# Constant rows copied by the engines that fill the first attention operands, and another order at the end of a four-stage transformer kernel

## The chip, the cores and the metric

The kernel runs on one core of a Trainium2 chip, as one program. A core has five engines that run their own instruction streams and wait for each other by semaphores: TensorE (PE, matrix products into PSUM, with its weight loads shown as PEld), VectorE (DVE), ScalarE (ACT), GpSimd (POOL) and SyncE (SP). SP, ACT and POOL also issue DMAs, and a DMA that waits for something holds up what its engine issues behind it. Sixteen transfer engines move the data of all queues. The metric is the time of one execution in microseconds (us), less is better.

## The reference

The input x holds 8 sequences of 512 tokens with 128 features, in fp32. Four stages follow each other, each with a sum of its input and its output and a layer norm behind it:

```
x = layernorm(x + attn0(x))   # 16 heads of 8; softmax(q k / sqrt(8) - slope_h |i - j|) v
x = layernorm(x + ffn0(x))    # silu(gate) * up, all operands quantised to FP4 in blocks of 16
x = layernorm(x + attn1(x))   # 16 heads of 8, without the distance term
x = layernorm(x + ffn1(x))
```

ffn1 is itself two layers. Each takes h, which is x with the second half of the features moved on by one token; makes q, k, v for 8 heads of 64; scales q and k to unit length, turns them with rotary tables; attends within a window of 64 tokens back; adds the projection to x; shifts again, normalises, and adds `(a * gelu(g)) @ w2 + b2` with `a, g` from one product of inner size 341 each.

## The kernel before, in words

**Stages and names.** x stays on the chip as xn and xs, 128 tokens a tile, four tiles (NT) a sequence, B = 8 sequences. Matrix products and transpositions of the attention are recorded by the helpers mm (L262) and tr (L263); the calls of the other engines show as L48 in the first stages and as L655 in ffn1, where the helper `kept` holds each engine to the program's order. `held` (L79) and `held_a` (L80) issue DMAs on SP's and ACT's queues in program order.

**The first attention's operands.** For each sequence there are two tiles q and k of 128 x 8 x 512 in the matrix format fp32r: eight pairs of heads in the middle dimension, and 64 partitions for each head of a pair (j = 0, 1). Of the 64 partitions, 0 to 31 hold data: the high and the low part of q and k, in the combinations whose products give an almost exact score. Partitions 32 to 47 hold constants that make the distance term, `rowq` and `rowk`; partition 63 holds a constant -1 in k and, in q, the largest score of each row, which is put there later (mt, by POOL's queue). The rest is zero. There are two sets: q0, k0 for even sequences and q1, k1 for odd ones.

Before the first sequence, `begin_x` transposes x (xt_ps, xT), `begin_qk` projects it for q and for k (qk_ps, x), POOL splits x in two parts, and SP writes these to a buffer in DRAM called far, two DMAs for each of q and k. `load_qk` reads them back spread over the partitions: 24 DMAs for q on SP and 24 for k on ACT. `begin_v` makes the values (va). Then the scores s_ps start: VectorE takes their row maxima m (sixteen large reductions for a group), these go back as mt, and a second product t_ps (the transposed scores), the exponential e and the product av with the values follow. A planner (`later`) hands the other sequences' operand steps, the bias row `crow` and the later stages' weights to numbered steps of this loop.

**The constants before.** DVE sets q0 to zero and POOL k0, while ACT's queue loads `raw`, 17 rows of 2 x 512; DVE casts it into rowq and rowk; then `constant_rows(0, held)` issues six DMAs on SP: row 63 of k, rows 32 to 47 of q and of k, for j = 0 and 1, each with its source broadcast over the eight pairs (16 KB or 256 KB written). They stand on SP's queue ahead of the far DMAs. `first_late`, called once when the first operands have been begun, does the same for q1 and k1: a memset on DVE and one on POOL, the values' ones (`filled`), six more row DMAs, and then `load_late`, the loads of x for sequences 2 to 7.

**The end of the last stage.** ffn1 has K = 16 items (layer times sequence) of NT = 4 chunks of 128 tokens: LAST = 64 chunks. A loop handles chunk t's projections together with the later steps of chunks t-1 to t-5: `operands_T` and `operands` (kT, qT copies), `scores` (sp), `maxima` (m), `weights` (pw, eight exponentials with sums on ACT), `over_sums` (POOL's product of pw with the reciprocal den), `weights_T` and `weights_taken` (p_ps, pT), `values` and `values_taken` (o_ps, oT), and `sums` (the products y_ps and their addition to xs by DVE). When an item's four chunks are summed, `shifted` (L709) builds hn, the shifted copy, by a small memset and four DMAs on SP (112 rows, 15 rows, the row that passes from a tile to the next, and the unshifted half); `normed` takes its moments (bn and st on DVE, rstd and mr on POOL) and adds the bias and x to xs (two POOL additions); `scaled` normalises hn; `turned` transposes it (nT); `gated` makes gelu and product of one of three parts (gp, ap, u); `sums(LAST, ..)` multiplies u by w2.

The loop leaves the last steps to a tail that is written out by hand (L1087 to L1148). In it E = 14 and L = 15 are the last two items. `rest(t)` issues the remaining steps of four chunks at once in a fixed order; `measured` and `finished` are the final layer norm of a sequence whose layer 1 is complete, with its output DMA.

```
E, L = K - 2, K - 1
rest(LAST)
sums(LAST - 5, LAST - 11)
begin_hn(E)
rest(LAST + 1)
normed(E)
...
begin_hn(L)
finished(E - 1 - B)
```

Of the kernel before, what the change touches and what calls it, by code (L numbers as in the profile page):

```python
# [9 lines left out]
F32 = mybir.dt.float32  # L10
F32R = mybir.dt.float32r
# [7 lines left out]
P = 128  # L19
B, S, D = 8, 512, 128  # L20
NT = S // P
# [30 lines left out]
def body(ctx, tc, x, consts, rows, wa0, wa1, acols, bo, wf, wqkv, wo, w1, w2, cols, b2r, qs, ks, out):  # L52
    nc = tc.nc
# [8 lines left out]
    rowq = outer.tile([16, S], F32R, name="rowq")  # L62
    rowk = outer.tile([17, S], F32R, name="rowk")
    sel = outer.tile([P, 2 * P], BF16, name="sel")
# [24 lines left out]
    dve.memset(half, -0.5)  # L89
    dve.memset(q0.bitcast(F32), 0.0)  # L90
    pool_.memset(k0.bitcast(F32), 0.0)
    with tc.tile_pool(name="rw", bufs=1) as once:
        raw = once.tile([17, 2, S], F32, name="raw")
        held_a(out=raw, in_=rows)
        held_a(out=wa[0], in_=wa0)
        held_a(out=acol, in_=acols)
        dve.tensor_copy(rowq, raw[0:16, 0, :])
        dve.tensor_copy(rowk, raw[:, 1, :])
    dve.tensor_tensor(qb, acol[:, :, 0], acol[:, :, 1], ALU.mult)
    dve.tensor_copy(sel, cst[:, C_SEL : C_SEL + 2 * P])  # L100
    dve.tensor_copy(tri, cst[:, C_TRI : C_TRI + P])
# [154 lines left out]
    def attention(li, alibi, qs_, ks_, va, batch, late=None, spare=None, alone=0):  # L256
# [7 lines left out]
        with ExitStack() as st:  # L264
# [137 lines left out]
            def plan():  # L402
# [34 lines left out]
                if not begun:  # L437
                    begin_x(0, batch[0])
                    begin_qk(0, batch[0], 0, held)
                    begin_qk(0, batch[0], 1, held)  # L440
                    begin_v(0, batch[0])
                    for part in (slice(0, 2), slice(2, 4), 1):
                        load_qk(0, batch[0], 0, part, held)
                        load_qk(0, batch[0], 1, part, held_a)
# [9 lines left out]
                if late:  # L454
                    late()
                if spare:
# [194 lines left out]
    def ffn1():  # L651
# [20 lines left out]
        LAST = NT * K  # L672
# [36 lines left out]

        def shifted(src, h):  # L710

            p_set(h[0:1, 0, 64:128], 0.0)
            for at, n in ((0, 112), (112, 15)):
                nc.sync.dma_start(out=h[at + 1 : at + 1 + n, :, 64:128], in_=src[at : at + n, :, 64:128])
            nc.sync.dma_start(out=h[0:1, 1:NT, 64:128], in_=src[P - 1 : P, 0 : NT - 1, 64:128])
            nc.sync.dma_start(out=h[:, :, 0:64], in_=src[:, :, 0:64])
            return h

        def rows_of(k):
            return slice((k % B) * NT, (k % B + 1) * NT)  # L720
# [70 lines left out]
        def main():  # L791
            with ExitStack() as st:
# [136 lines left out]

                def values_taken(k, c, h):  # L930
                    h["oT"] = work.tile([P, 4, P], F32, tag="oT", name="oT")
                    copy(h["oT"], h.pop("o"))

# [40 lines left out]

                def normed(k):
                    l, x = k // B, xs[:, rows_of(k), :]
                    item[k]["shape"] = moments(item[k]["hn"], "h")
                    p_tt(x, x, b2[:, l, :].unsqueeze(1).broadcast_to([P, NT, D]), ALU.add)
                    if l:
                        p_tt(x, x, xn[:, rows_of(k), :], ALU.add)  # L980
# [24 lines left out]
                def finished(b):  # L1005
                    x = slice(b * NT, (b + 1) * NT)
                    normalized(xs[:, x, :], xn[:, x, :], item[B + b].pop("shape"))
                    nc.sync.dma_start(out=ov[:, b], in_=xn[:, x, :])
# [67 lines left out]

                def rest(t):
                    at_(t - 4, weights_T)
                    at_(t - 3, over_sums)
                    at_(t - 4, weights_taken)  # L1080
                    at_(t - 2, scores)
                    at_(t - 2, maxima)
                    at_(t - 2, v_of)
                    at_(t - 1, operands_T)
                    at_(t - 1, operands)
                    at_(t - 4, values)
                    at_(t - 2, weights)  # L1087
                    at_(t - 4, values_taken)

                def begin_hn(k):  # L1090
                    hn = work.tile([P, NT, D], F32, tag="hn", name="hn", bufs=1)
                    item[k]["hn"] = shifted(xs[:, rows_of(k), :], hn)
# [40 lines left out]
                scaled(L)  # L1133
                for z in range(4):
# [20 lines left out]
    with tc.tile_pool(name="ops", bufs=1) as ops:  # L1155
        qs_, ks_ = ([at, ops.tile([P, 8, S], F32R, name=f"{n}1")] for n, at in (("q", q0), ("k", k0)))
        def constant_rows(i, start):
            for j in range(2):
                for t, at, src in ((ks_[i], 63, rowk[16:17]), (qs_[i], 32, rowq), (ks_[i], 32, rowk[0:16])):
                    n = src.shape[0]  # L1160
                    start(
                        out=t[64 * j + at : 64 * j + at + n].bitcast(F32),
                        in_=src.bitcast(F32).unsqueeze(1).broadcast_to([n, 8, S]),
                    )

        va = [va0, ops.tile([P, NT, 16, 32], F32, name="va1")]
# [49 lines left out]
        second, gates = [], []  # L1216
        constant_rows(0, held)
        psum = ExitStack()
# [25 lines left out]
def _constants():  # L1244
# [25 lines left out]
    at, blk = np.arange(S) - S // 2, np.arange(S) // 64  # L1270
    rows = np.zeros((17, 2, S), np.float32)
# [4 lines left out]
    rows[16, 1] = -1.0  # L1276
    return c, rows
# [55 lines left out]
```

## Time and profile before

The time is 1720.63 us, the median of three runs (1718.25 to 1721.07).

| what | value |
|---|---|
| profiled execution | 1720.81 us |
| its span, first to last instruction | 1719.0 us |
| mean granted TensorE clock | 0.972 |
| TensorE busy | 1620.5 us, 94% |
| VectorE busy | 1373.8 us, 80% |
| ScalarE busy | 1242.5 us, 72% |
| GpSimd busy | 911.6 us, 53% |
| moved by DMA | 90.25 MB, mean 53 GB/s |

Lines of a profile are read so. A line of the timeline or of the chain of waits gives the start in us from the start of the span, the length in us, the engine or DMA queue (SPq is SyncE's), the line of the code, and output<-input by the program's names; x4 means four such in a row, and brackets give the idle time before and what ended it. The chain of waits follows the work that ended last back through what released it. In a table by stretches, each engine has its busy time and number of instructions; then come TensorE's granted clock (1.00 is full), the busy share of the transfer engines and GB/s.

### The profile page before, as it was taken

How to read it: one execution, taken by the hardware profiler on the slowest of the kernel's cores; microseconds unless marked ns; L12 is line 12 of the kernel's file. 1: busy time of each engine (PE TensorE's matmuls, PEld its weight loads, DVE VectorE, ACT ScalarE, POOL GpSimd, SP SyncE). 2: the span in 40 equal slices, each digit the busy share in tenths (PEclk: the TensorE clock that was granted, in tenths of full speed). 3: DMA queues.
4: the chain of work that ended last, by engine and by line, in shares of the span. 5: the costliest groups of instructions: out<-in, count | busy, mean ns of one | idle time of the engine just before them, and what ended most of it. 6: DMA issues, size and time to landing. Idle time of an engine off the chain costs nothing.

```text
span 1719.0 us, 41770 instructions
## 1 busy us (share of the span) xinstructions
PE 1620.5 (94%) x16177; PEld 936.5 (54%) x16177; DVE 1373.8 (80%) x2177; ACT 1242.5 (72%) x2980; POOL 911.6 (53%) x976
## 2 busy tenths in 40 slices
PE   4999999999988799999999989999999999999995
PEld 2454555545546544444444446666666666666664
DVE  4788877888749878988889848888888888888863
ACT  1577776777755558887778767787888878888883
POOL 3323332232236741332332258888888888888873
PEclk7899999999999979999999999999999999999998
DMA  6725232221110243332332101111111111111110
GB/s 126 165 61 150 61 63 52 64 53 25 15 14 1 74 79 73 71 68 62 75 66 36 45 7 41 34 36 35 36 40 37 38 38 36 44 42 41 35 35 26
DMA packets 80777, 90.25 MB, mean 53 GB/s; under 512 B 46098, under 2 KB 58386, under 8 KB 76611
## 3 DMA queue, kind: packets, MB, share of 16 engines
q1 hardware_dynamic: 75504, 85.52, 23.2%
q8 instruction: 129, 2.11, 0.5%
q10 hardware_dynamic: 978, 1.52, 0.4%
q0 software_dynamic: 4096, 0.54, 0.3%
q14 instruction: 70, 0.57, 0.1%
HBM read 41.85 MB, written 18.87 MB: 35 GB/s over the span
## 4 chain that ended last, share of the span: by engine, by line
PE 78%; DVE 7%; POOL 5%; ACT 5%; issue 2%; DMA 2%; SPq 0%; DVEq 0%; POOLq 0%; ACTq 0%
PE av L262 16%; PE s_ps L262 13%; PE t_ps L262 10%; PE y_ps L655 5%; PE sp L655 5%; PE o_ps L655 3%; PE t_ps L655 3%; PE v_ps L655 3%; PE p_ps L655 3%; PE q_ps L655 3%; PE k_ps L655 2%; PE gp L655 2%; PE ap L655 2%; PE qk_ps L262 2%; ACT e L48 2%
## 5 line engine op out<-in xcount | busy, mean ns | idle before, releaser
L48 DVE TENSOR_REDUCE m<-s_ps 128x2 f32<-128x1024 f32 x512 | 620.4, 1223 | 140.7 <-PE s_ps L262 138.1
L48 ACT ACTIVATE e<-t_ps 128x512 f32<-128x512 f32 x1024 | 555.9, 596 | 166.1 <-PE t_ps L262 156.3
L262 PE MATMUL av<-e,va 128*32 128x256 f32 x4096 | 328.9, 394 | 6.8 <-ACT avs L48 6.8
L262 PE MATMUL s_ps<-k,q 63*128 63x512 f32 x1024 | 264.4, 510 | 21.5 <-DMA q<-far 15.1
L48 POOL DMA_DIRECT2D q<-mt x128 | 68.9, 542 | 347.7 <-ACT mt L48 347.3
L262 PE MATMUL t_ps<-q,k 64*128 64x512 f32 x1024 | 248.9, 447 | 1.3 <-ACT e L48 1.3
L655 ACT ACTIVATE pw<-sp,m,was_v 128x128 f32<-128x128 f32 x512 | 227.4, 480 | 1.5 <-DVE m L655 0.9
L262 PEld LDWEIGHTS s_ps<-k,q 63*128 63x128 f32 x1024 | 99.3, 188 | 228.3 <-issue 157.4
L655 POOL TENSOR_TENSOR was_v<-was_v 128x16 f32<-128x16 f32 x64 | 187.6, 2931 | 5.3
L262 PEld LDWEIGHTS t_ps<-q,k 64*128 64x128 f32 x1024 | 122.9, 189 | 23.7 <-ACT e L48 10.9
L262 PEld LDWEIGHTS av<-e,va 128*32 128x32 f32 x4096 | 81.6, 108 | 96.3 <-issue 62.7
L655 POOL TENSOR_TENSOR pw<-pw,den 128x1024 f32<-128x1024 f32 x64 | 121.2, 1894 | 9.3 <-DVE den L655 9.3
L655 ACT ACTIVATION_READ_ACCUMULATOR pw<-sp,m,was_v 128x1 f32 x512 | 116.5, 228 | 0.0
L262 PEld LDWEIGHTS <-sel 64*128 64x128 bf16 x2048 | 66.8, 97 | 76.4 <-issue 54.4
L655 DVE TENSOR_REDUCE m<-sp 128x4 f32<-128x512 f32 x128 | 82.2, 683 | 22.0 <-PE sp L655 20.2
L48 POOL CAST parts<-x 128x512 fp32r<-128x512 f32 x32 | 19.4, 608 | 139.8 <-ACT x L48 139.8
L655 POOL TENSOR_TENSOR was_k<-was_k,was_q 128x512 f32<-128x512 f32 x64 | 88.0, 1375 | 5.3 <-DVE was_q L655 5.3
L655 ACT COPY v<-v_ps 128x512 f32<-128x512 f32 x64 | 37.6, 588 | 72.3 <-PE v_ps L655 72.3
L655 PEld LDWEIGHTS t_ps<-cst,was_k 128*128 128x128 f32 x512 | 59.7, 142 | 43.1 <-issue 22.5
L655 DVE COPY pT<-p_ps 128x512 f32<-128x512 f32 x128 | 79.9, 664 | 0.5 <-PE p_ps L655 0.5
L655 PEld LDWEIGHTS p_ps<-cst,pw 128*128 128x128 f32 x512 | 59.8, 141 | 33.1 <-issue 27.8
L655 DVE TENSOR_REDUCE was_v<-was_k 128x16 f32<-128x1024 f32 x64 | 77.0, 1204 | 0.0
(191 smaller groups left out, 3223.1 us busy)
## 6 DMA issues: line engine op xcount, KB each, us to landing
far<-parts SPq DMA_DIRECT2D x64, 256.0 KB
q<-far SPq DMA_DIRECT2D x248, 64.0 KB
k<-far SPq DMA_DIRECT2D x240, 64.0 KB
ve<-v SPq DMA_DIRECT2D x112, 128.0 KB
xn<-in_x SPq DMA_DIRECT2D x8, 256.0 KB
q<-mt POOLq DMA_DIRECT2D x128, 4.0 KB, 3.0
hn<-xs SPq DMA_DIRECT2D x16, 128.0 KB
hn<-xs SPq DMA_DIRECT2D x16, 112.0 KB
```

What stands on the lines that cost most here:

```text
L48: return lambda *a, **k: self.tc.keep_in_program_order(f(*a, **k))
L262: mm = lambda *a, **k: tc.keep_in_program_order(nc.tensor.matmul(*a, **k))
L655: kept = lambda f: lambda *a, **k: tc.keep_in_program_order(f(*a, **k))
```

## The change

**Constants at the start.** The host's rows become 32 x 2 x 512 (sixteen constants, fifteen zero rows, and the last, -1 for k). The first 1024 columns of wqkv_s, a tile for weights that are loaded much later, serve as a buffer `fixed` of 128 x 2 x 512. DVE sets it to zero; ACT's queue loads the weights wa0, acol, crow, and then the rows twice, into partitions 32 to 63 and 96 to 127 of `fixed`. DVE copies its q half into q0, broadcast over the eight pairs (4096 elements a partition); ACT copies the k half into k0, between `begin_qk` and `begin_v`; POOL copies both into q1 and k1 in `late(True)`. rowk, the casts, the four memsets of the tiles and the twelve row DMAs are gone.

**The end of ffn1.** The `rest` calls are written out and reordered. The sum of chunk LAST-5 and hn's DMAs for E come ahead of the transposed operands of LAST-1; the weights of LAST-2 come ahead of kT and qT on ACT; the moments of hn(E) come behind the weights of LAST-1; one copy of oT goes to DVE; POOL's two additions for E (`based`) go behind `begin_hn(L)`; the four DMAs of hn(L) are split, two on SP and two on ACT's queue; and `finished` of sequence 5 goes behind the gelus of E.

```diff
-    dve.memset(q0.bitcast(F32), 0.0)
-    pool_.memset(k0.bitcast(F32), 0.0)
-    with tc.tile_pool(name="rw", bufs=1) as once:
-        raw = once.tile([17, 2, S], F32, name="raw")
-        held_a(out=raw, in_=rows)
-        held_a(out=wa[0], in_=wa0)
-        held_a(out=acol, in_=acols)
-        dve.tensor_copy(rowq, raw[0:16, 0, :])
-        dve.tensor_copy(rowk, raw[:, 1, :])
+    fixed = wqkv_s.rearrange("p l f -> p (l f)")[:, 0 : 2 * S].rearrange("p (n t) -> p n t", n=2)
+    dve.memset(fixed, 0.0)
+    held_a(out=wa[0], in_=wa0)
+    held_a(out=acol, in_=acols)
+    for j in range(2):
+        held_a(out=fixed[64 * j + 32 : 64 * j + 64], in_=rows)
+    filled_with = lambda e, t, n: e.tensor_copy(t, fixed[:, n, :].unsqueeze(1).broadcast_to([P, 8, S]))
     dve.tensor_tensor(qb, acol[:, :, 0], acol[:, :, 1], ALU.mult)
+    filled_with(dve, q0, 0)
...
                     begin_qk(0, batch[0], 1, held)
+                    late(False)
                     begin_v(0, batch[0])
...
-                    late()
+                    late(True)
...
-        def shifted(src, h):
+        def shifted(src, h, start=nc.sync.dma_start, other=None):
+            other = other or start
             p_set(h[0:1, 0, 64:128], 0.0)
-            for at, n in ((0, 112), (112, 15)):
-                nc.sync.dma_start(out=h[at + 1 : at + 1 + n, :, 64:128], in_=src[at : at + n, :, 64:128])
-            nc.sync.dma_start(out=h[0:1, 1:NT, 64:128], in_=src[P - 1 : P, 0 : NT - 1, 64:128])
-            nc.sync.dma_start(out=h[:, :, 0:64], in_=src[:, :, 0:64])
+            for at, n, by in ((0, 112, start), (112, 15, other)):
+                by(out=h[at + 1 : at + 1 + n, :, 64:128], in_=src[at : at + n, :, 64:128])
+            other(out=h[0:1, 1:NT, 64:128], in_=src[P - 1 : P, 0 : NT - 1, 64:128])
+            start(out=h[:, :, 0:64], in_=src[:, :, 0:64])
...
                 def normed(k):
+                    item[k]["shape"] = moments(item[k]["hn"], "h")
+                    based(k)
+
+                def based(k):
                     l, x = k // B, xs[:, rows_of(k), :]
-                    item[k]["shape"] = moments(item[k]["hn"], "h")
                     p_tt(x, x, b2[:, l, :].unsqueeze(1).broadcast_to([P, NT, D]), ALU.add)
...
                 E, L = K - 2, K - 1
-                rest(LAST)
+                at_(LAST - 4, weights_T)
+                at_(LAST - 3, over_sums)
+                at_(LAST - 4, weights_taken)
+                at_(LAST - 2, scores)
+                at_(LAST - 2, maxima)
+                at_(LAST - 2, v_of)
                 sums(LAST - 5, LAST - 11)
-                begin_hn(E)
-                rest(LAST + 1)
-                normed(E)
+                begin_hn(E, held)
+                at_(LAST - 1, operands_T)
+                at_(LAST - 2, weights)
+                at_(LAST - 1, operands)
+                at_(LAST - 4, values)
+                at_(LAST - 4, values_taken)
+                at_(LAST - 3, weights_T)
+                at_(LAST - 2, over_sums)
+                at_(LAST - 3, weights_taken)
+                at_(LAST - 1, scores)
+                at_(LAST - 1, maxima)
+                at_(LAST - 1, v_of)
+                at_(LAST - 3, values)
+                at_(LAST - 1, weights)
+                item[E]["shape"] = moments(item[E]["hn"], "h")
+                at_(LAST - 3, values_taken, v_copy)
+                sums(LAST - 4, LAST - 10)
+                turned_over(LAST - 2)
+                at_(LAST - 2, values)
+                at_(LAST - 1, over_sums)
+                at_(LAST - 2, values_taken)
                 scaled(E)
-                sums(LAST - 4, LAST - 10)
-                rest(LAST + 2)
                 sums(LAST - 3, LAST - 9)
-                measured(E - 1)
+                turned_over(LAST - 1)
                 turned(E)
                 turned_taken(E)
-                rest(LAST + 3)
+                at_(LAST - 1, values)
+                at_(LAST - 1, values_taken)
                 sums(LAST - 2, LAST)
                 sums(LAST - 1, LAST)
-                begin_hn(L)
-                finished(E - 1 - B)
+                begin_hn(L, held, held_a)
+                based(E)
+                measured(E - 1)
...
                 normed(L)
                 gated(E, 2)
+                finished(E - 1 - B)
                 scaled(L)
...
-        def first_late():
-            dve.memset(qs_[1].bitcast(F32), 0.0)
-            pool_.memset(ks_[1].bitcast(F32), 0.0)
+        def first_late(begun):
+            if not begun:
+                act_.copy(k0, fixed[:, 1, :].unsqueeze(1).broadcast_to([P, 8, S]))
+                return
+            filled_with(pool_, qs_[1], 0)
+            filled_with(pool_, ks_[1], 1)
             filled(va[1])
-            constant_rows(1, held)
             load_late()
...
-        constant_rows(0, held)
```

`turned_over(t)` is `weights_T` and `weights_taken` of chunk t. `constant_rows`, which only issued the row DMAs, is gone.

More of the change, by code (lines that the diff above doesn't have):

```diff
@@ L62, in body @@
     rowq = outer.tile([16, S], F32R, name="rowq")
-    rowk = outer.tile([17, S], F32R, name="rowk")
     sel = outer.tile([P, 2 * P], BF16, name="sel")
@@ L928, in values, with values_taken @@
                                 )
-                def values_taken(k, c, h):
+                def values_taken(k, c, h, by=copy):
                     h["oT"] = work.tile([P, 4, P], F32, tag="oT", name="oT")
-                    copy(h["oT"], h.pop("o"))
+                    by(h["oT"], h.pop("o"))
                 def sums(j, z):
@@ L1073, in main, with turned_over, begin_hn @@
                         finished(z // NT - 1 - B)
[L1077 to L1090, printed above, removed]
+                def turned_over(t):
+                    at_(t, weights_T)
+                    at_(t, weights_taken)
+                def begin_hn(k, *starts):
                     hn = work.tile([P, NT, D], F32, tag="hn", name="hn", bufs=1)
-                    item[k]["hn"] = shifted(xs[:, rows_of(k), :], hn)
+                    item[k]["hn"] = shifted(xs[:, rows_of(k), :], hn, *starts)
                 def scaled(k):
@@ L1156, in body @@
         qs_, ks_ = ([at, ops.tile([P, 8, S], F32R, name=f"{n}1")] for n, at in (("q", q0), ("k", k0)))
[L1157 to L1164, printed above, removed]
         va = [va0, ops.tile([P, NT, 16, 32], F32, name="va1")]
@@ L1270, in _constants @@
     at, blk = np.arange(S) - S // 2, np.arange(S) // 64
-    rows = np.zeros((17, 2, S), np.float32)
+    rows = np.zeros((32, 2, S), np.float32)
     for n in range(8):
@@ L1275, in _constants @@
         rows[n, 1], rows[8 + n, 1] = sign * at, -sign
-    rows[16, 1] = -1.0
+    rows[31, 1] = -1.0
     return c, rows
```

## The prediction

> **What bounds the kernel now.** I read the page's busy rows first, then the chain of waits at the two places that the change touches (the first 60 us and the last 65), then the timeline of each engine there. TensorE is busy nearly all of the span:
>
> ```profile
> PE 1620.5 (94%) x16177; PEld 936.5 (54%) x16177; DVE 1373.8 (80%) x2177; ACT 1242.5 (72%) x2980; POOL 911.6 (53%) x976
> ```
>
> So time is to be had only where TensorE waits. It does so at the start, where it ends its last projection at 14.9 us and has no scores until 27.9. The chain of waits says why (start us, length, what):
>
> ```profile
> 13.74 1.35 POOL parts L48 x2
> 15.10 7.21 DMA far<-parts
> 22.37 2.96 DMA q<-far
> 25.36 2.48 DMA q<-far
> 28.16 2.27 DMA q<-far
> 30.43 0.90 PE s_ps L262 x4
> ```
>
> The high and low parts of q and k go through DRAM (far) and back. 7.21 us for the way out is long. The SP queue and the transfer engines in the same stretch (timeline; then the table by stretches, whose last columns are granted clock, share of the transfer engines and GB/s):
>
> ```profile
> 9.19 2.54 SPq L79 DMA_DIRECT2D k<-rowk  x2
> 11.77 2.58 SPq L79 DMA_DIRECT2D q<-rowq  x1
> 14.39 0.60 SPq L79 DMA_DIRECT2D k<-rowk  x1
> 15.10 7.18 SPq L79 DMA_DIRECT2D far<-parts  x4
> ...
> 18.00:20.00 2.00, 0.00 (x0) 0.00 (x0) 0.00 (x0) 0.00 (x0) 2.00 (x1) 0.50 0.95 97
> ```
>
> Up to 15 us SP issues constant rows, and till about 20 us the engines are 0.95 busy at only 97 GB/s: that is the small packets of these rows, ahead of the far transfers. From 20 to 22 they move 222 GB/s.
>
> At the end of the program the chain leaves TensorE too:
>
> ```profile
> 1664.21 1.77 PE y_ps L655 x14
> ...
> 1668.36 3.15 DMA hn<-xs
> 1671.58 0.87 DVE bn L655 x4
> ...
> 1674.80 1.27 POOL xs L655
> 1676.15 1.27 POOL xs L655
> 1677.42 1.87 POOL pw L655
> ...
> 1684.86 0.38 SPq L1008
> ...
> 1687.04 2.36 DMA hn<-xs
> 1689.52 0.87 DVE bn L655 x4
> ...
> 1691.36 2.51 PE y_ps L655 x20
> ```
>
> **The start, part by part.** The sum is made against the profiled execution: 1720.81 us with a span of 1719.0 (1.8 around it), 0.2 above the median of 1720.63.
>
> *Removed:* twelve row DMAs on SP (six before far, 7.49 to 15.0; six at 40.3 to 49.1), two casts, four memsets of 3.5 us each. *Far:* the four issues start when parts are ready, at 15.10 as now, since POOL's parts do not move. Their issue costs 0.6 to 0.74 each without full queues in front (the later four, at 57.46, took 3.12 together; in front here they took 7.18). So k's first half is issued at about 16.95 (parts k ready) and lands 2.0 to 2.9 later, 19.6 to 20.5, where now it is 24.15; q's first load goes out at about 18.35 against 22.37. The k loads (24, on the ACT queue) and q loads keep their pace of 0.69 each. First scores earlier by **4.0 us**; 3 if the far transfers still queue behind late rows, 5 if they land at the quicker end.
>
> *Added:* the rows come by two DMAs of 128 KB on the ACT queue, behind the weights, acol and crow. The second waits for the weights to land (7.6 at the latest), so both are issued by 8.2. Their landing is not in the trace: 2.36 behind the issue by the last hn transfer above, 7.0 by xn's at the start, so 10.6 to 15.2. I take 10.6: xn's came when everything was loading at once, these come alone. Four copies of 4096 elements a partition follow. Nearest rows:
>
> ```profile
> 7.00 0.41 DVE L48 CAST rowk<-raw 17x512 fp32r<-17x512 f32 x1
> ...
> 1.68 3.47 DVE L48 MEMSET q<- 128x4096 f32 x1 [0.82 <-issue]
> ...
> 42.30 0.58 ACT L48 COPY xT<-xt_ps 128x512 f32<-128x512 f32 x1 [26.70 <-PE xt_ps L263]
> ...
> 13.05 0.61 POOL L48 CAST parts<-x 128x512 fp32r<-128x512 f32 x1 [6.81 <-ACT x L48]
> ```
>
> DVE's q0: 2.2 us by the slope of its casts (0.41 for 512, 0.22 for tri's 128), 3.5 by the memset. It ends at 12.8 to 14.1 and q's loads need it at 18.3; with rows at 15.2 it ends at 17.4 to 18.7, which costs 0.4 at most. sel, tri and bvb stand behind it on DVE (0.7 together); the first scores' correction needs them at 24: hidden. ACT's k0: 0.58 for 512 elements and 0.25 for mt's 128 (at 43.42) give 3.7, and 4.6 if nothing of the 0.58 is fixed; I take the slope. It stands behind x(k), at 14.6, so it ends at 18.3 to 19.2, and va's two copies (0.65) behind it go to 19.9. The k loads, issued by ACT itself, start when k's first far half lands, at 19.6 to 20.5: hidden, at the upper end lost by 0.3. Rows at 15.2 put it 0.6 later. Each microsecond beyond is lost. POOL's q1 and k1: 4.9 each by its cast (3.5 memset; 10.2 by its 1.27 us subtraction), then va1's 2.07: 16.9 to 28.7, at most 39.4. POOL's next work is the adds of xs and crow at 33.4, which nothing reads soon, and the q<-mt issue at 40: hidden, at the upper end by 0.6.
>
> ACT's table load (1.28) now stands behind the second rows DMA: it ends at 8.2 to 9.5 and xT is due at 9.46. 0 to 0.1 lost; up to 1.2 gained if xn lands sooner. I take 0.
>
> Everything from the first scores to the tail keeps its order on each engine, so the 4.0 is carried through. q1 and k1 rows leaving SP at 40 to 49 removes only transfers that TensorE did not wait for: 0.
>
> **The tail, part by part.** I walked each engine's new order with the present durations.
> 1. y(LAST-5) goes ahead of a transposition that waits for POOL, into TensorE's idle time: ends 1662.3 instead of 1665.97. xs follows at 1662.3, and the four hn(E) DMAs go out 1662.65 to 1665.7, landing 1667.4 to 1668.2 (now 1671.51).
> 2. DVE has the maxima of LAST-1 until 1668.6 first, so bn(E) starts then: -3.0 against 1671.58. A wait less on DMA, one more on DVE.
> 3. The two POOL adds (1.27 each) move behind hn(L). So POOL's pw(LAST-1) starts at 1673.05, when ACT's weights are done, instead of 1677.38: -4.3.
> 4. TensorE has o(LAST-2) and y(LAST-3) until 1675.85, then p(LAST-1): -3.5 against 1679.33. xs of the last chunk ends near 1680.9 against 1684.8: -3.9.
> 5. hn(L): two DMAs on SP, two on ACT, 1680.95 to 1682.35; landed 1684.3 to 1685.05 against 1689.43.
> 6. Behind ACT's two issues (0.66 and 0.77 by today's like ones) stand the table load and the gelus: gelu at 1683.65, u1 until 1685.75. So bn(L) starts at 1685.75 against 1689.52, u2 ends 1687.6 against 1691.3, y(E) starts 1687.65 against 1691.36: **-3.7 us**.
>
> ```profile
> 1684.75 1.28 ACT L655 ACT_TABLE_LOAD   x1
> 1686.05 0.69 ACT L655 ACTIVATE u<-gp,cols_s 128x512 f32<-128x512 f32 x1
> ```
>
> The load here ends 0.02 before the gelu, so 1.28 is its whole price. The Trainium skill, "ScalarE: Activation LUTs", section "What ACT_TABLE_LOAD costs", adds a drain of about 1.4 us to each switch; in that case step 6 would end 1.4 later and the tail give -2.3. The trace shows no such drain, so the sum goes by the row.
>
> The moved adds (2.54) fall in POOL's idle stretch before rstd(L); the moved xn of finished (1.65) falls behind the gelus and ends 0.3 before hn(L) is ready to be scaled; if not, 0.5 is lost. Bounds of the tail: -2.5 (hn at its slow landing, 3.15, and finished in the way) to -4.5 (steps 3 and 5 without the gelus' limit). After 1691 the order is unchanged.
>
> Sum: 1720.81 - 4.0 - 3.7 = **1713.1 us**.
>
> **The rivals.**
> *The clock's phase.* TensorE had half clock to 48.1, full clock to 54.95, half again to 61.8, while busy throughout in that last stretch:
>
> ```profile
> 48.10:51.50 3.40, 2.58 (x20) 1.00 (x19) 3.33 (x4) 0.69 (x1) 2.57 (x3) 1.00 0.92 104
> ...
> 54.95:58.40 3.45, 3.45 (x28) 2.47 (x30) 2.60 (x3) 2.12 (x6) 2.31 (x6) 0.50 1.16 297
> ```
>
> Steps lie 6.8 us apart. Work moved by 4.0 meets them elsewhere. A half-clock stretch of 6.8 holds 3.4 us of full-clock work: without it 1709.7, with one more 1716.5. For more: the full clock came only after 41.3 to 48.1 was wholly busy; moved by 4.0, that stretch takes in the gaps now at 50 to 52. Against a full 3.4: from 47 to 55 DVE is busy with maxima almost without a break, so a slower TensorE costs little there. The Trainium skill, "TensorE: Matmul & The Clock Gate", Part 1, says the window is free-running, some 3.4 us, and one busy window is enough; by that the clock could come back a window sooner. In the trace 41.3 to 44.7 was wholly busy and the clock stayed at half, so the case of more is likelier.
>
> *The start is hidden by something else* (rows that land only at 19, so that k0's 3.7 and va end near 23.4; or far slow by itself): only the tail counts, 1717.1. Against it: 97 GB/s ahead of far and 222 to 281 when it runs.
>
> *The tail is given back*: the table load or hn landing sets step 6 as late as now; 1716.8. For it: ACT's issues are a new wait in front of the load.
>
> *Slower.* ACT's k0 copy runs far under its rate. Every microsecond past 20 delays the k loads, which ACT issues, and so the scores. With 7.7 to make up it must end, va included, past 27.7, so take over 12.4 us, more than three times the estimate; 16 us gives 1724.4. The rows of ACT at 512 elements speak against it; none is fp32r at this length.
>
> *The change does less than it says*: a second queue for hn(L) saves issue time only, 1.4, which is in step 5 already and is not the limit; without it step 6 is the same.
>
> **How the numbers follow.** Forecast 0.55 (its own range 1711.3 to 1715.3, from 3 to 5 at the start and 2.5 to 4.5 at the end); clock with less 0.08, with more 0.14; start hidden 0.09; tail given back 0.07; slower 0.07. To leave out no more than 2 in 10, the range takes in both clock cases and reaches to the hidden start: 1709.7 to 1717.1. A measurement of this kernel can tell about 0.2% from no change, 3.4 us: below 1717.2 is faster. Half of "start hidden" and a little of the clock and tail cases fall above it: faster 0.84, same 0.09, slower 0.07.
>
> **What would show it.** Right: far<-parts x4 issued in about 3.2 us; q<-far from 18.3; first s_ps near 24; k0's copy under 4.4 and done before far lands; bn(E) near 1664.6 and y(E) near 1683.6 in the new trace (both 4.0 less by the start). Wrong: an ACT copy that ends past 20; POOL still copying at 33; the half clock past 48; ACT's table load later than its queue entries above; hn(L) landing last before bn(L).

## The result and the profile after

The changed kernel takes 1714.07 us (median of six runs, 1713.37 to 1715.24) against 1720.76 for the one before (median of six); the ratio is 0.9959, with a 95% interval of 0.9945 to 0.9973, or 7.1 us less with bounds of 4.6 and 9.5. The profiled execution of the changed kernel is its slowest: 1715.24 us, with a span of 1713.5. Against the span of before that is 5.5 less. The medians lie 6.7 apart. The two traces show where the 5.5 us of these two executions come from.

The chain of waits of the changed kernel at its start (start us, length, what):

```profile
1.19 3.69 DMA xn<-in_x
...
9.73 1.30 POOL parts L48
...
14.36 3.90 DMA far<-parts
...
19.75 2.71 DMA k<-far
22.48 2.38 DMA k<-far
24.89 0.45 DMA k<-far
25.34 0.89 PE s_ps L261 x4
...
26.25 3.50 DVE m L48 x3
```

Two lines of the same chain in the kernel before:

```profile
1.20 7.00 DMA xn<-in_x
...
31.35 3.50 DVE m L48 x3
```

In the changed kernel the scores start at 25.34 and not at 30.43: 5.1 us earlier (one product ahead of them runs at 22.91, in before at 27.93). Three things differ from the chain of before. x lands at 4.88 instead of 8.20. The first of POOL's parts takes 1.30 instead of 0.62. And the far stretch is 3.90 instead of 7.21, after which the loads of k, no longer those of q, set the scores.

The timeline of the changed kernel (start, length, engine):

```profile
8.25 2.29 DVE L48 CAST q<-wqkv_s 128x4096 fp32r<-128x4096 f32 x1 [3.40 <-DMA wqkv_s<-in_rows]
...
9.73 1.29 POOL L48 CAST parts<-x 128x512 fp32r<-128x512 f32 x1 [6.59 <-ACT x L48]
...
10.90 3.60 ACT L48 CAST k<-wqkv_s 128x4096 fp32r<-128x4096 f32 x1
...
14.27 3.61 POOL L48 CAST q<-wqkv_s 128x4096 fp32r<-128x4096 f32 x1
...
12.45 3.15 SPq L78 DMA_DIRECT2D far<-parts  x4
```

The four far DMAs are issued in 3.15 us where they took 7.18, and each of the copies has a length: 2.29 on DVE, 3.60 on ACT, 3.61 on POOL. POOL's cast of 512 elements takes 1.29 instead of 0.61 while DVE copies beside it.

Not all of the 5.1 us is kept in this execution. The table by stretches of the changed kernel (last three columns: granted clock, transfer share, GB/s):

```profile
44.70:48.10 3.40, 1.92 (x22) 1.27 (x21) 3.13 (x3) 0.51 (x1) 1.89 (x2) 0.90 0.60 154
48.10:51.50 3.40, 3.40 (x27) 2.69 (x25) 2.81 (x3) 1.61 (x4) 0.00 (x0) 0.50 0.73 195
51.50:54.95 3.45, 3.45 (x28) 2.39 (x32) 2.38 (x2) 2.13 (x6) 2.46 (x6) 0.50 0.52 100
54.95:58.40 3.45, 3.45 (x29) 1.34 (x22) 1.29 (x2) 1.81 (x4) 0.28 (x1) 0.50 0.56 107
58.40:61.80 3.40, 3.40 (x28) 2.46 (x28) 0.69 (x1) 0.90 (x3) 0.00 (x0) 0.61 0.34 68
```

TensorE is busy without a gap from 48 to 62 and has half clock for nearly all of it; in before it had half clock for 6.8 us there. The first maxima are 5.10 earlier than before (26.25 against 31.35). The copy of the values of the chunk before last, the last thing ahead of the tail, is 2.53 earlier. ACT's timeline, first of the kernel before, then of the changed one:

```profile
1660.57 0.58 ACT L655 COPY v<-v_ps 128x512 f32<-128x512 f32 x1 [0.55 <-PE v_ps L655]
...
1658.04 0.59 ACT L655 COPY v<-v_ps 128x512 f32<-128x512 f32 x1 [0.54 <-PE v_ps L655]
```

In between, the distance of like instructions of DVE and ACT does not simply shrink once. It is 2.3 us at 65, 1.0 near 590, 4.5 near 640, 5.3 near 1020, and 2.6 from 1100 on; it hardly moves in the long stretches at full clock (65 to 490, 640 to 1010, 1100 to 1660) and changes where one trace or the other has half clock, and shortly behind. The mean granted clock up to the tail is 0.97 in both. So the 5.10 at the start and the 2.53 at the end are linked by several gains and losses, and not by the stretch behind the scores alone.

The chain of waits in the tail of the changed kernel:

```profile
1676.34 2.00 PE y_ps L655 x16
1678.36 0.30 DVE xs L655
1678.73 1.06 ACTq L79
1679.83 0.75 ACTq L79
1680.61 1.28 ACT L655
1681.90 0.70 ACT u L655
...
1683.34 0.70 DVE u L655
1684.04 0.78 DVE bn L655 x4
```

The landing of hn is gone from the chain, and so are POOL's two additions. ACT's two DMA issues (1.06 and 0.75), then its table load (1.28; the line of ACT behind the issues), then the gelu stand in their place. From the copy of the values named above to the start of ACT's last group of instructions it is 44.15 us (1658.04 to 1702.19) where it was 47.18 (1660.57 to 1707.75): the tail gained 3.0.

### The profile page after: what moved, and what is told of

It reads as the page before. It is cut to its first block, busy times and chain, and to the rows that moved or that the text cites. A ratio compares the mean times of both kernels' runs of the same rounds, so it can differ in the third digit from the quotient of the medians.

```text
span 1713.5 us, 41753 instructions
## 1 busy us (share of the span) xinstructions
PE 1618.2 (94%) x16176; PEld 936.9 (55%) x16177; DVE 1372.4 (80%) x2176; ACT 1246.7 (73%) x2980; POOL 914.1 (53%) x976
## 3 DMA queue, kind: packets, MB, share of 16 engines
q0 software_dynamic: 4096, 0.54, 0.3%
## 4 chain that ended last, share of the span: by engine, by line
PE 78%; DVE 8%; ACT 5%; POOL 4%; issue 2%; DMA 1%; ACTq 0%; SPq 0%; DVEq 0%; POOLq 0%
PE av L261 16%; PE s_ps L261 13%; PE t_ps L261 10%; PE y_ps L655 5%; PE sp L655 5%; PE o_ps L655 3%; PE t_ps L655 3%; PE v_ps L655 3%; PE p_ps L655 3%; PE q_ps L655 3%; PE k_ps L655 3%; PE gp L655 2%; PE ap L655 2%; PE qk_ps L261 2%; POOL y L483 2%
```

## The experiments

Times are medians; each ratio is to runs of the kernel before on the same chip, with its 95% interval. The kernel before spread from 1714.4 to 1725.1 us over these runs, so the ratios carry the comparisons, and the traces show where a difference lies. The last column is from one execution of each kernel. There, the four kernels with exactly the start of the changed one (changed, start only, early table, hn(L) all on SP) range from 26.25 to 27.11.

| kernel | us | ratio to before | first maxima at, us |
|---|---|---|---|
| before | 1720.76 | 1 | 31.35 |
| changed kernel | 1714.07 | 0.9959 [0.9945, 0.9973] | 26.25 |
| start only | 1715.06 | 0.9974 [0.996, 0.9988] | 27.11 |
| tail only | 1717.84 | 0.9978 [0.9965, 0.9991] | 31.65 |
| before, raw over 32 rows | 1721.49 | 0.9998 [0.9983, 1.0014] | 30.41 |
| changed, copy after the parts | 1715.27 | 0.9964 [0.9951, 0.9978] | 27.03 |
| changed, rows ahead of acol | 1713.88 | 0.9937 [0.9919, 0.9955] | 27.74 |
| changed, TensorE kept busy | 1711.23 | 0.9945 [0.9929, 0.9962] | 26.08 |
| changed, TensorE filled | 1712.51 | 0.9934 [0.9912, 0.9957] | 25.93 |
| changed, early table | 1711.03 | 0.994 [0.9921, 0.9959] | 26.34 |
| changed, hn(L) all on SP | 1712.38 | 0.9945 [0.9931, 0.9958] | 26.87 |
| rows, filling and early table | 1708.76 | 0.9914 [0.9899, 0.9928] | 27.32 |
| kept busy and early table | 1711.71 | 0.9943 [0.993, 0.9957] | 25.97 |
| filled longer and early table | 1706.83 | 0.9914 [0.99, 0.9927] | 26.12 |

### The two parts, each alone

The first kernel has the constants of the change and the tail of before; the second has the start of before and the new tail.

> Only the constants at the start are changed, the tail is that of before. If the two parts add up, the start gives what the tail does not: the tail's own gain in the trace of after is 3.0 us (the shift against before goes from -2.5 at 1659 to -5.56 at the end), so this kernel should be 3.7 faster than before, near 1717.0, with first scores near 25.3 us of the span. Rival, the clock eats the start (a second half-clock stretch behind the scores): 1719 to 1720.8, within 2 us of before.

> Only the tail is changed. If the tail's gain is its own, 3.0 us: 1717.7, with y(E) 3.0 earlier behind the last v_ps than before. Rival, the tail gains only because the start moved the clock's phase or the queues: within 1 us of before.

By the ratios the start gives 4.5 us (2.1 to 6.9) and the tail 3.8 (1.5 to 6.0), together 8.3 where the whole change gave 7.1: they add up within their intervals, and by them both rivals fall. The tail's trace says it more sharply: from the same copy of the values to ACT's last group 44.21 us (1664.45 to 1708.66), against 47.18 before and 44.15 with both parts. It also shows how far two traces of the same program drift: up to that copy this kernel is the one before, and yet the copy comes 3.9 later than in before. The profiled execution of the start alone took 1718.64, above its median: it had the first maxima 4.24 earlier, and the second half-clock stretch as well. Its POOL and DVE lines (timeline of the kernel with the start only):

```profile
9.59 2.50 POOL L48 CAST parts<-x 128x512 fp32r<-128x512 f32 x1 [6.46 <-ACT x L48]
...
9.33 2.29 DVE L48 CAST q<-wqkv_s 128x4096 fp32r<-128x4096 f32 x1 [4.83 <-DMA wqkv_s<-in_rows]
```

Here the rows landed a microsecond later than in the changed kernel, though the start is the same; DVE's copy began 1.1 later, and POOL's cast of 0.6 took 2.5, since the copy covered nearly all of it.

### What let x land earlier

One thing is changed in before: raw is padded from 17 rows to 32.

```diff
-        raw = once.tile([17, 2, S], F32, name="raw")
+        raw = once.tile([32, 2, S], F32, name="raw")
...
-    rows = np.zeros((17, 2, S), np.float32)
+    rows = np.zeros((32, 2, S), np.float32)
```

> Before, with one thing changed: raw is loaded as 32 rows of 4 KB and not 17, fifteen of them zeros. If the load over 17 partitions is what kept xn until 8.20 (transfer share 0.39 and then 0.11 from 6 to 9 us, a few engines left with long work), xn lands near 4.9 and the first transposition starts 3.3 earlier; the constant rows on SP still stand ahead of far, so the scores come at most 3.3 earlier, 30.4 less 0 to 3.3. Time 1717.5 to 1720.8. Rival, it was the rows' place ahead of the weights: xn lands at 8 again and nothing moves.

Chain of waits, then SP's timeline, of this kernel:

```profile
1.19 4.02 DMA xn<-in_x
...
18.91 4.29 DMA far<-parts
...
29.48 0.91 PE s_ps L262 x4
...
14.27 7.13 SPq L79 DMA_DIRECT2D far<-parts  x4
```

x lands at 5.21 instead of 8.20, although more bytes are loaded ahead of it. So it was the shape of the load, 17 partitions, that held x back. The Trainium skill, "DMA: Bandwidth & Descriptors", section "Why a DMA increments its semaphore by 16 and not by 1", says that a DMA uses the largest number of transfer engines up to 16 that divides its slowest dimension, and that 127 partitions get one engine. By that rule 17 rows go through one engine and 32 through sixteen. The transfer share of 0.11 between 7 and 9 us in before, 1.8 of sixteen engines, fits a few engines with long work, and does not count them; with 32 rows the share between 7 and 8 is 0.00. The scores move only 0.95 us, since the far DMAs still take 7.13 to issue behind the rows, and the time doesn't move at all. The early x is worth something only once the rows are out of SP's queue; in the changed kernel both hold.

### DVE's copy and POOL's parts

Two ways to keep DVE's copy of q0 away from POOL's casts. The first puts the loads of the rows ahead of acol's, which was meant to bring the copy forward; the second holds the copy back until POOL has done its parts.

```diff
+    for j in range(2):
+        held_a(out=fixed[64 * j + 32 : 64 * j + 64], in_=rows)
     held_a(out=acol, in_=acols)
-    for j in range(2):
-        held_a(out=fixed[64 * j + 32 : 64 * j + 64], in_=rows)
```

```diff
-    filled_with(dve, q0, 0)
...
                     late(False)
+                    seen = const.tile([P, 1], F32, name="seen")
+                    dve.tensor_copy(seen, batch[0]["parts", 1][:, 1, 0:1].bitcast(F32))
+                    filled_with(dve, qs_[0], 0)
```

> After, with the two loads of the constant rows ahead of the load of acol on ACT's queue, so that acol and not the second rows load waits for the weights to land. If DVE's copy of q0 (8.25 to 10.54) is what stretches POOL's first cast from 0.61 to 1.29, an earlier copy leaves the cast at 0.6: k's parts end 0.7 earlier, first scores 0.7 earlier, near 24.6, time 0.7 less, 1713.4 by that alone. Rival, the cast is long for another reason (first use of its tile or of its kind): 1.29 again, scores at 25.3, 1714.0.

> After, with DVE's copy of q0 held back until POOL has made the last part of k (a copy of one column of that part stands in front of it). If DVE's copy is what stretches POOL's first cast (1.29 in after, 2.51 where both ran side by side in full, 0.62 where the copy was earlier), the cast is 0.6, parts of k end 0.7 earlier, and the copy itself (2.3) still ends before q's loads can go: first scores 0 to 0.8 earlier. Rival, the loads of q then wait for the copy: scores up to 1.5 later.

The first kernel, chain and POOL's timeline:

```profile
1.19 6.11 DMA xn<-in_x
...
12.15 0.61 POOL L48 CAST parts<-x 128x512 fp32r<-128x512 f32 x1 [9.01 <-ACT x L48]
```

The second, timeline of POOL, DVE and SP:

```profile
9.80 0.61 POOL L48 CAST parts<-x 128x512 fp32r<-128x512 f32 x1 [6.67 <-ACT x L48]
...
17.15 5.66 POOL L48 CAST k<-wqkv_s 128x4096 fp32r<-128x4096 f32 x1
...
13.82 5.54 DVE L48 CAST q<-wqkv_s 128x4096 fp32r<-128x4096 f32 x1
...
19.39 10.56 SPq L78 DMA_DIRECT2D q<-far  x17
```

In both, the cast is back at 0.61, so the stretch is DVE's copy and nothing about the cast itself. Neither brings the scores earlier. In the first both loads of rows go out while x is loaded, x lands at 7.30, and POOL's parts start 2.4 later (first maxima 27.74); DVE's copy, which there waits for acol, runs from 9.64 and is done before the cast. In the second the copy meets POOL's copies of q1 and k1 instead: 5.54 where it takes 2.29 alone, POOL's 5.66 where it takes 3.60, and q's loads wait for it until 19.39 (15.79 in the changed kernel). The rival of the second run held, and its first maxima are 0.8 later than in the changed kernel. By its ratio the first kernel is nevertheless not slower than the changed one (the intervals overlap); its profiled execution had no second half-clock stretch and full clock from 46 to 490 us, and whether the shift of the start brings that about each time is open. The place that the change chose, into the start of POOL's parts, costs 0.7 to 1.9 us of the cast. Its first maxima (26.25) are the earliest of the three places in these traces, but with the same start they came at 26.87 and 27.11 in two other kernels, no earlier than the 27.03 of the second; so no order of these two places is shown.

The ends of the rows say what the longer durations are. The cast ends 0.48 behind DVE's copy in the changed kernel (11.02 and 10.54) and 0.47 behind it in the kernel with the start only (12.09 and 11.62). In the second kernel here DVE's copy ends 2.15 behind POOL's copy of q1 (13.61 to 17.21), and POOL's copy of k1 ends 3.45 behind DVE's. Each remainder is nearly the instruction's own time alone (0.61, 2.29, 3.60). So these rows look like the one that comes second waiting until the first is done, and not like both running slower.

The Trainium skill, "GPSIMD Engine Reference", section "1. Specifications", has it that POOL shares its ways into SBUF with VectorE, and contends with VectorE's instructions that use two ports or two inputs there. The durations of this copy agree: the cast takes 0.61 alone, 1.29 and 2.50 beside it. DVE's memset of before, which ended at 13.49 while POOL's cast of 13.05 still took 0.61, did not hold it up. Whether the copy is of the kind that uses two ports, no run here shows.

### The clock

After the values, TensorE multiplies ten times into a bank that nobody reads, in the time in which it would idle.

```diff
                     begin_v(0, batch[0])
+                    idle = p_av.tile([P, S], F32, tag="av", name="idle")
+                    for _ in range(10):
+                        mm(idle, lhsT=w[:, 0:P], rhs=batch[0]["xT"], start=True, stop=True)
```

> After, with ten more products of the first projection into an unused bank between the values and the first scores, results unread, so that TensorE does not idle from 11.2 to 22. If the clock's phase took 2.8 of the 5.1 us gained at the first scores, keeping the full clock over the idle time should give that back and more: the scores' stretch at full clock, 1711.3 by 2.8 back, down to 1708 if the wholly busy stretch at half clock halves too. Rival, gaps between the scores drop the clock again within 7 us: 1713 to 1715, as after.

Table by stretches of this kernel:

```profile
24.00:26.00 2.00, 0.85 (x9) 0.68 (x9) 0.00 (x0) 0.00 (x0) 0.00 (x0) 0.78 0.39 109
26.00:34.00 8.00, 6.39 (x41) 3.33 (x37) 7.77 (x8) 0.00 (x0) 1.70 (x4) 0.50 0.50 98
34.00:42.00 8.00, 7.80 (x39) 3.91 (x37) 5.42 (x6) 1.62 (x3) 1.41 (x3) 0.50 0.67 107
42.00:50.00 8.00, 6.62 (x58) 3.38 (x56) 8.00 (x8) 2.62 (x5) 3.67 (x4) 0.99 1.12 311
```

The clock still falls, near 25, when the scores begin with their gaps; but it comes back at 42, and no second half-clock stretch follows up to 489 us. The time is 1711.23, the expected 2.8 less than the changed kernel, though the intervals of the two ratios overlap. That points to the clock as what took the start's gain back. The executions point the same way, clock and time going together: of the 23 executions of the kernel before that stand beside this run's the quickest, 1714.96 us, had a mean granted clock of 0.977 and the slowest, 1725.1, one of 0.970; with the start only the ends are 1711.48 at 0.978 and 1722.11 at 0.969. And the gaps between 20.5 and 25, 4.1 us in two pieces, were enough to lose it. The next run also filled those gaps, and the steps of the first group:

```diff
-                    for _ in range(10):
+                    for _ in range(13):
                         mm(idle, lhsT=w[:, 0:P], rhs=batch[0]["xT"], start=True, stop=True)
+                    for at in range(16):
+                        later(at, lambda: mm(idle[:, 0:256], lhsT=w[:, 0:P], rhs=w[:, 0:256], start=True, stop=True))
```

> After, with thirteen unread products in the idle time ahead of the scores and one of half the size in each of the first sixteen steps, 0.44 us each at full clock, in gaps that end on DVE's maxima. If only the clock makes the first group of scores slow (48.31 for the first t_ps, 25.34 for the scores), full clock from 11 to 50 leaves it bound by DVE, 16 maxima of 1.17, 18.7 us: first t_ps near 45, shift against before near -8 at 53 and -10 at 65 instead of -3.9 and -2.3. Time about 1709. Rival, the filling takes TensorE's time and the clock falls anyway: 1711 to 1715.

Its table by stretches:

```profile
20.80:24.20 3.40, 2.31 (x6) 0.72 (x4) 0.00 (x0) 0.00 (x0) 2.72 (x4) 1.00 0.38 102
24.20:27.70 3.50, 2.35 (x17) 1.30 (x17) 1.76 (x2) 0.00 (x0) 0.00 (x0) 0.98 0.41 119
27.70:31.10 3.40, 3.40 (x16) 1.81 (x16) 2.36 (x3) 0.00 (x0) 0.00 (x0) 0.50 0.54 94
31.10:34.50 3.40, 3.40 (x14) 1.92 (x12) 2.21 (x3) 0.00 (x0) 0.00 (x0) 0.50 0.50 77
```

In this execution the rival held: TensorE was busy for 2.31 and 2.35 of two stretches of 3.4, the clock fell at 27.6, and at half clock the filling then makes TensorE the bound (DVE only 2.2 to 2.4 busy of 3.4), so that the first exponential came at 54.30, later than in before (53.34). TensorE stayed at half clock for 17 us, up to 44.7, although it was busy without a gap from 27.7. The Trainium skill, "TensorE: Matmul & The Clock Gate", Part 1, has the full clock back after one busy window of 3.4 us; here five such windows did not do it, and the measurement decides. What does decide the return is left open. The profiled execution is this kernel's slowest, 1716.97 at a granted clock of 0.979; the quickest of the four is 1706.98 at 0.984. Where the clock falls thus differs from run to run; that the place of the gaps decides it is not shown.

### The tail's limit

A gelu of one element a partition behind ACT's last oT copy moves the table load in front of ACT's two issues.

```diff
                 at_(LAST - 1, values_taken)
+                early_gelu = work.tile([P, 1], F32, tag="early_gelu", name="early_gelu", bufs=1)
+                act(early_gelu, half[:, 0:1], AF.Gelu)
```

> After, with a gelu of one element a partition behind ACT's last oT copy, so that the table is loaded before ACT's two hn issues and not behind them. If the load behind the issues (1680.61, 1.28) sets the gelus, u and bn(L), the first gelu comes 1.3 earlier and bn(L) 1.0 earlier, when hn lands (issue end 1680.58 plus 2.36): 1713.0. Rival, hn's landing is the limit by itself: no change, 1714.0.

ACT's timeline of this kernel:

```profile
1674.88 1.28 ACT L655 ACT_TABLE_LOAD   x1
1676.18 0.20 ACT L655 ACTIVATE early_gelu<-half 128x1 f32<-128x1 f32 x1
1676.63 1.84 ACTq L79 DMA_DIRECT2D hn<-xs  x2
1678.52 1.27 ACT L655 ACTIVATE u<-gp,cols_s 128x512 f32<-128x512 f32 x2 [2.14 <-PE ap L655]
```

The gelus now start right behind the issues. From the copy of the values (1655.94) to ACT's last group (1698.80) it is 42.86 us: 1.3 less than in the changed kernel, near the 1.0 expected. So the load behind the issues was the limit, and hn's landing was not.

> After, with the four DMAs of hn(L) all on SP as in before, none on ACT. If the split over two queues is what makes hn(L) land earlier, it is lost: ACT's table load and gelus come 1.9 earlier, but SP issues until about 1681.3 instead of 1680.1 (with the span's time of after), hn lands 2.4 later, near 1683.7, and bn(L) starts there against 1683.95: no change, 1713.8 to 1714.3. Rival, ACT's two issues in front of the load cost more than the split saves: bn(L) at 1682.7 or earlier, 1 us less.

```diff
-                begin_hn(L, held, held_a)
+                begin_hn(L, held)
```

SP's and DVE's timeline of the kernel with all four DMAs on SP:

```profile
1678.62 3.15 SPq L78 DMA_DIRECT2D hn<-xs  x4
...
1683.63 0.88 DVE L655 BATCH_NORM_STATS2 bn<-hn 128x6 f32<-128x128 f32 x4 [1.09 <-DMA hn<-xs]
```

bn(L) waits for hn again and starts at 1683.63, beside 1683.95 in the changed kernel. From the copy of the values to ACT's last group it is 43.92 us (1657.95 to 1701.87), 0.2 less. The median, 1712.38, lies below the expected range, but the intervals of the two ratios overlap. The split of hn(L) over two queues, then, gave nothing by itself: what it took off SP it put in front of ACT's table load. Counted from the copy of the values, bn(L) comes at 24.62 us with the split and the early table (1680.56) and at 25.68 here, where hn's landing sets it. So the split should be worth about 1.1 once the load is out of the way; that is an estimate from these two rows, and no run has the early table without the split.

### Put together

> After, with the rows ahead of acol, TensorE filled as in the run beside it, and the early gelu table. If the three are independent: 0.7 + 1.7 (the early table in the trace: tail -4.73 against -3.04) + 3 to 6 of the clock below 1714.07, so 1706 to 1709. Rival, the clock's phase absorbs what the start gains: 1709 to 1712.

> After, with the ten unread products and the early gelu table together. If the two add up: 1714.07 less 2.8 (1711.23 with the products) less 1.7 (the early table in the trace): 1709.5. Rival, the clock's spread hides one of them: 1711.

> After, with sixteen unread products in the idle time (until 25.8, behind the landing of the first k loads), one of half the size in each of the first sixteen steps, and the early gelu table; the rows stay behind acol. If the full clock holds as in the run with the three together, where no half-clock stretch came before 499 us, and the scores start 1.5 to 2 earlier than there, 1706.5 to 1707.5. Rival, the clock falls at about 27 as where thirteen products were used, and the filling then costs TensorE's time: 1711 to 1713.

(The 1.7 that these expectations take for the early table is too much; its size is the 1.3 above.) The three together reached 1708.76, at the upper end of what was expected if they are independent, with full clock up to 495 us, though its first maxima are 1.1 later than in the changed kernel for the rows ahead of acol. Ten products and the early table came to 1711.71 where 1709.5 was expected of their sum. In its trace the tail keeps the early table's gain (42.8 us from the copy of the values, 1655.78 to 1698.62), and the clock falls twice before 60 us, as in the changed kernel: the rival describes the trace, but the interval of the ratio takes in the sum too. The last kernel has sixteen products, until the first loads of k have landed, the small ones in the first sixteen steps, and the early table. It has the lowest median, 1706.83; its ratio of 0.9914 (0.99 to 0.9927) is that of the three together, and the interval lies wholly below that of the changed kernel. Its table by stretches:

```profile
20.80:24.20 3.40, 3.40 (x10) 1.49 (x9) 0.00 (x0) 0.00 (x0) 2.77 (x4) 1.00 0.38 110
24.20:27.70 3.50, 3.50 (x20) 1.55 (x18) 1.58 (x2) 0.00 (x0) 0.00 (x0) 1.00 0.40 119
...
48.10:51.50 3.40, 3.12 (x36) 1.68 (x35) 3.23 (x3) 2.58 (x7) 1.73 (x4) 1.00 0.60 161
```

TensorE has no gap until 48, and the clock stays full up to 485 us. All four executions of this kernel had a granted clock of 0.984 to 0.986, all four of the three together 0.985, where the six of the changed kernel had 0.972 to 0.973.

## Why the prediction was right, and where its steps were off

The time (1713.1 forecast, 1714.07 measured) and the sign came out, and both places gave what they were to give in kind. The closeness of the number is in part luck: the traces have 5.1 at the start for 4.0 and 3.0 at the tail for 3.7, and the clock took 2.6 of it in the profiled execution, so that 5.5 are left there for a forecast of 7.7. The steps one by one:

- **What bounds the start** was read rightly: rows ahead of far. With the rows gone the four far issues took 3.15 us (3.2 forecast). Padding raw alone, with the rows still on SP, let x land 3 earlier and left the time where it was.
- **"POOL's parts do not move" failed.** They moved by 2.6 us (k's last part ends at 14.33, not 16.90), because x landed 3.3 earlier. The prediction had priced that landing at 0, with 1.2 as the bound, and only for ACT's table load: raw's load of 17 rows does not stand in its list of what is removed. So q's loads, forecast from 18.35, began at 15.79. Of the 3.3, POOL's stretched cast took back 0.7.
- **The far landing** of k took 3.9 from the start of its issue (14.36 to 18.26), above the 2.65 to 3.55 that the forecast's times mean (16.95 to 19.6 and 20.5); why is open. The parts 2.6 earlier less this landing 0.4 to 1.3 longer would make 5.3 to 6.2 of the 4.0; the first scores came 5.1 earlier.
- **The copies.** DVE 2.29 (2.2), ACT 3.60 (3.7). POOL's 3.61 were put at 4.9 by its cast; the 3.5 of its memset of the same shape was the nearer row. The rows landed by 8.25, before the 10.6 taken. That DVE's copy holds up POOL's cast was not foreseen at all; it is a wait on the path that the change added.
- **"Everything from the first scores to the tail keeps its order ..., so the 4.0 is carried through"** is the weakest step. The order did hold, but in the profiled execution the distance did not: 5.10 at the first maxima were 2.53 at the tail. The rival of the clock's phase, in its dearer form (one more half-clock stretch of 6.8 us), had named it at 3.4 and a chance of 0.14; behind the first scores it came about (5.10 down to 2.3 by 65 us), and with it the sign "the half clock past 48". That the distance at the tail is again near 2.3 is chance, since later stretches took and gave up to 3.5 in between. How much of the start's gain is kept on average is open: the start alone gave 4.5, with 2.1 to 6.9 in its interval. That the clock is the cause is shown best by the last run, in which TensorE was filled and the clock stayed full: there the distance to before grew from 5.23 at the first maxima to 8.6 at 65 us, where it fell to 2.3 in the changed kernel. Those 6.3 us are about what the two ratios differ by (7.7) less the early table's 1.3. Its further growth to 11.14 at the tail (the copy of the values at 1649.43) comes for the most part between 600 and 640, as the changed kernel's from 1.0 to 4.5 does.
- **The tail.** Steps 1 to 4 came within 0.3 us: bn(E) at 1666.39 (forecast 1666.1, moved to this span), pw(LAST-1) on POOL at 1670.67 (1670.5), the end of the last xs at 1678.65 (1678.4). Step 6 was mis-sized: ACT's two issues took 1.85 and not 1.43, and with the 0.3 from the last xs the gelu came 0.8 late, and the tail gave 3.0 and not 3.7. "Behind ACT's two issues stand the table load and the gelus" was the right limit, as the early table shows. That a second queue for hn(L) is not the limit, as the last rival had it, the run with all four on SP bears out.
- **The table load's price.** It ended 0.01 before the gelu in the changed kernel too (1680.61, 1.28, then 1681.90). No run shows the drain of about 1.4 us that the Trainium skill, "ScalarE: Activation LUTs", section "What ACT_TABLE_LOAD costs", adds; here the load is 1.28 in all.
- The slower rival did not come near: ACT's copy kept the rate of its short copies.

## What to carry to other kernels

A gain in a stretch where TensorE waits is not safely carried through later busy stretches: the clock keeps its own time, so look at the granted clock behind the place, and consider work without a reader to bridge a long idle time. Count a DMA by the engines that its outermost dimension lets it use and by what stands behind it in the queue, and a copy on DVE by what POOL does beside it. Before reading a difference of a few us off two traces, look at how far traces and times of one kernel lie apart. A wait that is moved off a DMA queue onto a computing engine's queue lands in front of that engine's next work, a table load for instance, which can be drawn forward.

## What the hardware showed that was not expected

- A load of 17 rows of 4 KB delayed x, loaded beside it, until 8.20 us; 32 rows of 4 KB, almost twice the bytes, let it land at 5.21.
- DVE's copy of 4096 fp32 elements a partition takes 2.29 us alone and 5.54 beside POOL copies of the same shape, the second of which goes from 3.60 to 5.66; a POOL cast of 0.61 goes to 1.29, and to 2.50 where the copy covers it. In each case the later one ends about its own time alone behind the end of the earlier.
- With unread products bridging 12 to 26 us, and small ones after that, the clock stayed full to 485 us; with 2.3 busy of 3.4 us in two stretches running it fell to half, and it stayed there for 17 us although TensorE was busy throughout.
